# Two state-space layers, one core: second delta and second projection of the next scan moved beside the output pipeline, with DVE additions

## The chip, the cores and the metric

One core of one Trainium2 chip runs the whole batch of 8 images. The metric is the time of one execution on the device in microseconds (us), the median of several runs. The engines are PE (matrix products into PSUM, with PEld for its weight loads), DVE (vector), ACT (scalar functions and copies), POOL (GpSimd, elementwise here) and SP, which issues nearly all DMAs of this kernel. Every engine and SP work through their own queue in order.

## The reference

Two layers follow each other on x of shape (8, 64, 64, 96). Both normalise by groups, project to 2 x 192 channels, convolve 3x3 by channel, apply SiLU, scan the 4096 positions in four directions, normalise over channels, gate with SiLU(z), project back to 96 and add x. Layer 0's scan is the expensive one:

```
xs    = cross_scan(xc)                       # 4 directions: rows, columns, both reversed
x_dbl = einsum('bkdl,kcd->bkcl', xs, x_proj_w)   # 6 delta rows, 16 B rows, 16 C rows
delta = softplus(x_dbl[:, :, :6] projected to 192 channels + dt_projs_b)
dA    = exp(delta * A)                       # A: 192 channels x 16 states per direction
h     = dA * h + delta * B * u               # along 4096 positions
y     = sum over 16 states (h * C) + u * D
y     = layernorm(merge of the 4 directions); out = x + (y * silu(z)) @ out_proj_w.T
```

Layer 1 is the same in shape, with shared weights for the directions and a scan in closed form, of which only the first 160 positions of each direction contribute (a check at the end falls back to a general form).

## The kernel before

**Tiling.** Channels lie on partitions in two halves (h = 0, 1) of 96, positions in pieces of T = 1024. The scan of an image runs over 4 directions x 4 pieces = 16 *units*; a unit has 2 *jobs* (one per half), a job 3 groups of 32 channels, a group 4 *sets* of 128 partitions (32 channels x 4 states). That is 768 wide instructions `tensor_tensor_scan` on DVE per image, each 128x1024. For images 1 to 7 a short unit (24 short sets) follows that serves layer 1 of the image before.

**What a job needs.** `projection` (per unit) multiplies xc with the projection weights into 78 rows, `take` copies them out of PSUM, and a DMA stores them (x_dbl); `replicate` reads B and C rows back, each broadcast to 128 partitions (512 KB a transfer). `ready` (per job) makes delta as a softplus in two parts: `argument` (2 matmuls from the first 7 rows of x_dbl), `parts` (Relu and Abs), `exponential`, `rounded` and `rounding` (the rounding error of 1 + z, by two Identity passes), `logarithm`; then `total` adds the four terms z, dtu, ln and dt on PE as products with the unit matrix (4 per half tile, 8 per job), `delta` copies the sum back into `ln`, POOL's `product` makes delta x u, `store` writes both to DRAM, and `fetch` reads them back broadcast (dt_rep, dtu_rep). For units of the reversed directions `low_rows` reads the 7 rows back from DRAM instead of projecting again.

**Order inside the scan.** `scan_rows` writes the order by hand: step n issues one set's instructions for every engine, set n's scan on DVE, set n+1's decay on ACT, set n+5's fetch on SP, and so on, and then the stages of `plan[n]`. Steps -5 to -1 fill the pipe. Job m+2 and unit m/2+2 are prepared while job m runs, so two jobs and two units must be ready at the beginning: job 0 and unit 0 come from outside (`first_delta`), job 1 and unit 1 are made by `early_steps` in steps -5 to 1 of the scan itself.

**Order between scans.** `between(b, y)` runs `out_phase` on one or two streams of 8 chunks: the finish of layer 0 of image b and, from b = 1, the finish of layer 1 of image b-1, whose input y1 `short_sum` reads back from DRAM (8 loads), scales on ACT and patches on DVE. A chunk passes fixed lags: sum (0), mean on PE and `centre` on DVE (1), `square` (2), variance (3), gates and SiLU (7), `row` and `scale` (8), affine and product (9), output projection and `end` (10). After each step's stages come those of `plan[k]`, filled by `put(step, stage)`. Beside the chunks the plan holds: the four loads of the next image's xc, the first projection and first delta of the next scan (`first_delta`, steps 3 to 18), the statistics of x of image b+2 (`piece` loads and `chunk_stats`, then the three stages of a group norm at steps 10, 11, 14) and the group norm of layer 1 (18, 19, 20). Every fourth step also has `newton` on DVE and `roots` on ACT for the inverse deviation. PSUM tiles of `mean`, of `weights` and of all beside work share two banks. Image 0 has no pipeline before it: `begin` runs the same stages one after the other.

SP issues loads and stores of all these stages in one queue.

Of the kernel before, what the change touches and what calls it, by code (L numbers as in the profile page):

```python
# [10 lines left out]
ALU = mybir.AluOpType  # L11
# [36 lines left out]
def two_ss2d_layers(ctx: ExitStack, tc: tile.TileContext, t: dict, out: bass.AP):  # L48
# [352 lines left out]
    def scan_rows(xc, y, parts, plan, beside):  # L401

        with (
            tc.tile_pool(name="piece", bufs=1) as piece,
            tc.tile_pool(name="work", bufs=2) as work,
            tc.tile_pool(name="pslot", bufs=2, space=PSUM) as pslot,
            tc.tile_pool(name="pdrive", bufs=1, space=PSUM) as pdrive,
            tc.tile_pool(name="pacc", bufs=1, space=PSUM) as pacc,
            tc.tile_pool(name="pmisc", bufs=1, space=PSUM) as pmisc,
        ):
            units, jobs, sets, x_dbl = parts  # L420
            total = len(sets)
            plan = plan(pmisc)
            with tc.manual_schedule():
                low_rows(x_dbl, units[0], piece)
                state = None

                stages = ready(xc, x_dbl, jobs[1], piece, pmisc)
                stages += projection(xc, x_dbl, units[1], piece, pmisc)
                early_steps = (-5, -5, -5, -5, -4, -4, -4, -3, -3, -2, -2, -1, 0, 1)
                for step, (_, stage) in zip(early_steps + (-4, -3, -3, -2), stages):  # L430
                    plan.setdefault(step, []).append(stage)
                for n in range(-AHEAD, max(total + 4, max(plan, default=0) + 1)):
                    at = lambda i: sets[n + i] if 0 <= n + i < total else None
                    m, j = divmod(n + 1, PER)
                    if j == 0 and 0 <= m < len(jobs):

                        stages = []
                        if m + 2 < len(jobs):
                            prepare = short_ready if jobs[m + 2]["unit"]["short"] else ready
                            stages += prepare(xc, x_dbl, jobs[m + 2], piece, pmisc)  # L440
                        if m % NH == 1 and m // NH + 2 < len(units):
                            unit = units[m // NH + 2]
                            project = short_projection if unit["short"] else projection
                            stages += project(xc, x_dbl, unit, piece, pmisc)
                        for step, stage in stages:
                            plan.setdefault(n + step, []).append(stage)
                    fetch(at(AHEAD), work)
                    replicate(at(AHEAD_BC), x_dbl, work)
                    if at(0) and at(0)["unit"]["nth"] == 0 and at(0)["first"]:
                        state = piece.tile([P, D // GC * NS], F32, name="state0", bufs=2)  # L450
                    advance_set(at(0), state, work)
                    keep_state(at(-1))
                    fill(at(1), pslot)
                    if n % NS == NS - 2:
                        drive(at(2), pdrive)
                    release(at(-4), y, beside)
                    gate(at(1), work)
                    read_out(at(-1), work)
                    early(at(2), work)
                    collect(at(-3), xc, y, pacc)  # L460
                    for stage in plan.pop(n, []):
                        stage()
                assert not plan
# [26 lines left out]
    def low_rows(x_dbl, unit, piece):  # L490

        k, t0 = unit["k"], unit["t0"]
        unit["x_dbl"] = piece.tile([2 * ROWS, T], F32, name="x_dbl0")
        src = x_dbl[k % 2][k // 2 * ROWS :, t0 : t0 + T]
        nc.sync.dma_start(unit["x_dbl"][: R + 1, :], src[: R + 1, :])
# [36 lines left out]
            (4, lambda: take(1)),  # L532
        ]

    def ready(xc, x_dbl, job, piece, pmisc):

        unit, h = job["unit"], job["h"]
        k, t0, col = unit["k"], unit["t0"], unit["column"]
# [46 lines left out]
        def delta(s):  # L585
            nc.scalar.copy(job["ln"][:, halves[s]], job["ps"][:C, :])  # L586
            if s == SUB - 1:
                job["dt"] = job["ln"]

        def product():  # L590
            nc.gpsimd.tensor_tensor(  # L591
                like(job["dtu"], col),
                like(job["dt"], col),
                positions(xc[:, h, :], col, t0, T),
                ALU.mult,
            )

        def store():
            for c in ("dt", "dtu"):
                job[f"{c}_far"] = dram.tile([C, T], F32, name=f"{c}_far", bufs=3)  # L600
                nc.sync.dma_start(job[f"{c}_far"], job[c])

        return [
            (0, lambda: argument(0)),
            (1, lambda: parts(0)),
# [3 lines left out]
            (4, rounded),  # L609
            (5, rounding),  # L610
            (6, logarithm),
            (10, lambda: total(0)),
            (11, lambda: delta(0)),
            (11, lambda: total(1)),
            (12, lambda: delta(1)),
            (13, product),
            (15, store),
        ]
# [935 lines left out]
                chunk_stats(st, i, piece)  # L1554
        return group_norm(st, bank)

    def first_delta(b, xc, pool, pfirst):

        units, jobs, sets, x_dbl = parts = scan_parts(b)
        stages = projection(xc, x_dbl, units[0], pool, pfirst)  # L1560
        stages += ready(xc, x_dbl, jobs[0], pool, pfirst)
        return parts, [stage for _, stage in stages]

    def begin():

        with tc.tile_pool(name="pfirst", bufs=2, space=PSUM) as pfirst:
            bank = lambda name: pfirst.tile([P, MM], F32, tag="mm", name=name)
            xc = keep.tile([C, NH, L], F32, name="map")
            with tc.tile_pool(name="first", bufs=1) as pool:
                norm0[0] = conv_first(t["x"][0], xc, pool, bank)  # L1570
            with tc.tile_pool(name="before", bufs=1) as pool:
                parts, stages = first_delta(0, xc, pool, pfirst)
                for stage in stages:
                    stage()
            if NB > 1:
                norm0[1] = first_norm(1, bank)
        return xc, parts
# [11 lines left out]
    def short_sum(b, pool, put):  # L1589

        y1 = pool.tile([C, NH, L], F32, name="y1")
        ys = pool.tile([C, NH, HN], F32, name="ys")

        def load(h, i):
            at = slice(i * T, (i + 1) * T)
            nc.sync.dma_start(y1[:, h, at], xc1_far[b][:, h, at])

        def scale(h, i):
            at = slice(i * T, (i + 1) * T)
            nc.scalar.mul(y1[:, h, at], y1[:, h, at], w["dsum1"][:, h : h + 1])  # L1600

        def patch(h):
            for k, at, dst in segments(y1[:, h, :]):
                part = shaped(ys[:, h, k * HEAD + at.start : k * HEAD + at.stop], dst)
                nc.vector.tensor_tensor(dst, part, dst, ALU.add)

        put(0, nc.sync.dma_start, ys, ys_far[b])
        for h in range(NH):
            for i in range(NT):
                put(0, load, h, i)  # L1610
                put(4 + 2 * h + i // 2, scale, h, i)
            put(6 + h, patch, h)
        return y1

# [12 lines left out]
    def between(b, y):  # L1627
# [3 lines left out]
        with (  # L1631
# [11 lines left out]
            if b >= 1:  # L1643
                streams.append(second_of(b - 1, pool, put))
            for i in range(1, NT):
                put(7 + i, load, i)
            found = {}

            def beside(pmm):
                bank = lambda name: pmm.tile([P, MM], F32, tag="mm", name=name)  # L1650
                found["parts"], stages = first_delta(b + 1, xc, before, pmm)
                steps = (3, 4, 4, 5) + (5, 6, 6, 7, 10, 11, 11, 14, 15, 16, 16, 17, 17, 18)
                for step, stage in zip(steps, stages, strict=True):
                    put(step, stage)
                stages, found[1] = group_norm_stages(st, bank)
                for step, stage in zip((18, 19, 20), stages):
                    put(step, stage)
                if b + 2 < NB:
                    ahead = stats_tile()
                    pieces = []  # L1660

                    def piece(i):
                        pieces.append(before.tile([C, MM], F32, name="x_st", bufs=3))
                        nc.sync.dma_start(pieces[i], t["x"][b + 2][:, i * MM : (i + 1) * MM])

                    for i in range(L // MM):
                        put(i, piece, i)
                        put(i + 2, lambda i: chunk_stats(ahead, i, pieces[i]), i)
                    stages, found[0] = group_norm_stages(ahead, bank)
                    for step, stage in zip((10, 11, 14), stages):  # L1670
                        put(step, stage)
                return plan

# [163 lines left out]
```

## Time and profile before

| what | value | from |
|---|---|---|
| median of 3 runs | 12977.52 us (12971.58 to 12991.91) | times |
| the profiled execution | 13001.91 us, span of its instructions 13000.0 | times, page |
| busy, share of the span | DVE 87%, POOL 83%, ACT 75%, PE 75% | page, part 1 |
| granted TensorE clock, mean | 0.785 | table of cores |
| output pipelines behind images 0 to 7 | 82.8, 166.7, 164.2, 164.1, 163.6, 164.6, 145.4, 124.0 us | table by stage |
| one scan instruction 128x1024, one product set x B on DVE | 2.35 and 1.18 us | page, part 5 |

Busy time counts instructions at work; the mean over the span mixes the scans, where DVE and POOL are full, with the stretches between them. The times of the pipelines run from the first y_sum (line 1480) to the last result on DVE (line 1583 or 1531). The page's chain of waits holds only the very last pipeline and says nothing on the seven passages from image to image.

### The profile page before, as it was taken

The numbers are of one execution on the slowest core, as the hardware profiler recorded it, in microseconds if no ns is written. First come the engines' busy times: TensorE is split into PE (matmuls) and PEld (weight loads), VectorE is DVE, ScalarE is ACT, GpSimd is POOL, SyncE is SP. The second block draws the span as 40 slices with busy tenths as digits, with TensorE's granted clock in tenths as the row PEclk, the third lists the DMA queues.
The fourth block names the chain that finished last, engine by engine and source line by source line (L and its number), as shares of the span: only waits on it lengthen the run. The fifth ranks groups of instructions, "written<-read, shape, count | busy, mean of one in ns | idle before, by whom it ended". The sixth has DMA issues, their size and how long they took to land. (4 is left out here: it accounts for less than half of the span.)

```text
span 13000.0 us, 135568 instructions
## 1 busy us (share of the span) xinstructions
PE 9704.7 (75%) x44540; PEld 3050.4 (23%) x44540; DVE 11319.6 (87%) x7485; ACT 9795.9 (75%) x14884; POOL 10736.0 (83%) x4883
## 2 busy tenths in 40 slices
PE   6875688876888678876788867888588785886556
PEld 2221222222222222222222212222122221222112
DVE  6999799996999969999699996999869998799976
ACT  4788688776787768877688776887678886788864
POOL 4999798985999859898699976999769997799964
PEclk8887787877887778787788777888688886887766
DMA  3444444443444434444344434444344444344430
GB/s 98 159 159 153 131 161 155 158 148 100 161 157 158 145 107 162 151 159 140 119 161 158 157 123 124 161 158 157 119 125 161 157 162 129 132 160 156 155 96 25
DMA packets 654249, 1839.49 MB, mean 141 GB/s; under 512 B 174856, under 2 KB 178318, under 8 KB 653437
## 3 DMA queue, kind: packets, MB, share of 16 engines
q1 hardware_dynamic: 653533, 1830.73, 42.1%
q8 instruction: 353, 5.78, 0.2%
q14 instruction: 363, 2.97, 0.1%
HBM read 1524.94 MB, written 305.52 MB: 141 GB/s over the span
## 5 line engine op out<-in xcount | busy, mean ns | idle before, releaser
L842 POOL TENSOR_TENSOR out<-set,c_rep 128x1024 f32<-128x1024 f32 x3240 | 7471.5, 2326 | 941.2 <-PE acc L866 315.9
L825 DVE TENSOR_TENSOR_SCAN set<-decay,state,set 128x1024 f32<-128x1024 f32 x2304 | 5366.1, 2345 | 430.1 <-ACT decay L780 209.5
L780 ACT ACTIVATE decay<-dt_rep,w_a 128x1024 f32<-128x1024 f32 x3240 | 3553.1, 1097 | 559.5 <-DVE set L825 319.5
L814 DVE TENSOR_TENSOR set<-drive,b_rep 128x1024 f32<-128x1024 f32 x2430 | 2865.7, 1179 | 103.8 <-ACT drive L797 88.2
L866 PE MATMUL acc<-out,w_gather 128*32 128x256 f32 x25920 | 2398.8, 482 | 544.6 <-ACT y_short L886 393.5
L934 PE MATMUL ps_conv<-edged,taps 96*96 96x512 f32 (+1 forms) x4032 | 2461.4, 750 | 28.2 <-ACT z L558 26.0
L804 POOL TENSOR_TENSOR set<-dtu_rep,b_rep 128x1024 f32<-128x1024 f32 (+1 forms) x810 | 1898.5, 2344 | 56.0 <-DMA dt_far<-ln 29.8
L825 DVE TENSOR_TENSOR_SCAN set<-decay,set 128x1024 f32<-128x1024 f32 x768 | 1744.0, 2286 | 212.1 <-ACT decay L780 132.4
L857 PE MATMUL acc<-map,w_eye 96*32 96x256 f32 x4608 | 565.5, 572 | 1480.0 <-ACT map L897 1245.9
L897 ACT COPY map<-acc 32x256 f32<-32x256 f32 x3072 | 1471.0, 479 | 48.8 <-PE acc L866 8.6
L866 PEld LDWEIGHTS acc<-out,w_gather 128*32 128x32 f32 x25920 | 841.4, 132 | 2528.5 <-issue 1474.0
L591 POOL TENSOR_TENSOR dtu<-ln,map 96x1024 f32<-96x1024 f32 x256 | 670.5, 2619 | 481.4 <-ACT ln L586 303.1
L934 PEld LDWEIGHTS ps_conv<-edged,taps 96*96 96x96 f32 (+1 forms) x4032 | 722.4, 199 | 1362.7 <-issue 1209.0
L836 ACT COPY state<-set 128x1 f32<-128x1 f32 x2304 | 426.2, 185 | 753.9 <-DVE set L825 746.5
L577 PE MATMUL ps_sp<-z,w_eye 96*96 96x512 f32 x1024 | 700.5, 772 | 341.3 <-ACT ln L586 257.9
L797 ACT COPY drive<-dtu_rep 128x1024 f32<-128x1024 f32 (+1 forms) x810 | 797.0, 984 | 15.4 <-DVE set L814 10.9
L545 PE MATMUL ps_dt<-x_dbl,w_dtw 7*96 7x512 f32 x1024 | 590.3, 657 | 189.8 <-ACT z L558 157.3
L577 PE MATMUL ps_sp<-dtu,w_eye 96*96 96x512 f32 x1024 | 605.1, 676 | 0.7 <-ACT dtu L572 0.7
L577 PE MATMUL ps_sp<-ln,w_eye 96*96 96x512 f32 x1024 | 578.9, 650 | 0.0
L586 ACT COPY ln<-ps_sp 96x512 f32<-96x512 f32 x512 | 297.4, 581 | 347.8 <-PE ps_sp L577 340.7
L857 PEld LDWEIGHTS acc<-map,w_eye 96*32 96x32 f32 x4608 | 101.3, 121 | 1934.9 <-ACT map L897 1635.7
L577 PE MATMUL ps_sp<-dt,w_eye 96*96 96x512 f32 x1024 | 543.2, 613 | 0.0
(224 smaller groups left out, 9645.6 us busy)
## 6 DMA issues: line engine op xcount, KB each, us to landing
dt_rep<-dt_far SPq DMA_DIRECT2D x768, 512.0 KB, 4.0
dtu_rep<-dtu_far SPq DMA_DIRECT2D x768, 512.0 KB, 5.2
b_rep<-x_dblr SPq DMA_DIRECT2D x256, 512.0 KB, 7.7
c_rep<-x_dblr SPq DMA_DIRECT2D x256, 512.0 KB, 7.3
b_rep<-x_dblc SPq DMA_DIRECT2D x256, 512.0 KB, 8.0
c_rep<-x_dblc SPq DMA_DIRECT2D x256, 512.0 KB, 6.8
dt_far<-ln SPq DMA_DIRECT2D x256, 384.0 KB, 3.6
dtu_far<-dtu SPq DMA_DIRECT2D x256, 384.0 KB, 3.0
```

Of the source, the lines that this page charges most:

```text
L577: nc.tensor.matmul(job["ps"][:C, :], w["eye"], job[term][:, halves[s]], start=i == 0, stop=i == 3,)
L591: nc.gpsimd.tensor_tensor(like(job["dtu"], col), like(job["dt"], col), positions(xc[:, h, :], col, t0, T), ALU.mult,)
L780: nc.scalar.activation(s["decay"], s["group"]["dt"], AF.Exp, scale=rate)
L797: nc.scalar.copy(s["group"]["drive"], s["group"]["dtu"])
L804: nc.gpsimd.tensor_tensor(s["buf"], s["group"]["dtu"], b, ALU.mult)
L814: nc.vector.tensor_tensor(s["buf"], s["group"]["drive"], b, ALU.mult)
L825: nc.vector.tensor_tensor_scan(ordered(s["buf"], unit), ordered(s["decay"], unit), ordered(s["buf"], unit), 0.0 if unit["nth"] == 0 else s ...
L842: nc.gpsimd.tensor_tensor(s["out"], s["buf"], s["unit"]["c", s["i"]], ALU.mult)
L857: nc.tensor.matmul(acc, lhs[:, GC * g : GC * (g + 1)], positions(old[:, h, :], unit["column"], unit["t0"] + at, n), start=True, stop=False ...
L866: nc.tensor.matmul(acc, w["gather"], s["out"][:, at : at + n], start=s["i"] == 0 and unit["short"], stop=s["i"] == NS - 1, skip_group_chec ...
L897: nc.scalar.copy(yk, like(acc, unit["column"]))
L934: nc.tensor.matmul(job["ps"][:C, :], taps[l][:k, h, tap, :], edged[:k, tap // 3 : tap // 3 + rows, tap % 3 : tap % 3 + WW], start=tap == 0 ...
```

## The change

`first_delta` becomes `first_deltas`: beside the output pipeline it now makes the first projection, the first delta, the second delta and the second projection. In all deltas made there `ready(..., by_pe=False)` replaces the four stages `total(0)`, `delta(0)`, `total(1)`, `delta(1)` by one, `sums`, three additions on DVE. `scan_rows` loses `early_steps`; it reads the 7 rows of the second unit's x_dbl back from DRAM (`low_rows`, first stage of step -1). Later deltas inside the scan still go by PE. In the pipeline, the loads of `short_sum` move from step 0 to 1 and 2, its scalings to other steps, the loads of xc from 8, 9, 10 to 8, 10, 12, the pieces of x and their statistics six steps back, and their group norm to steps 16, 17, 18.

```diff
@@ scan_rows
-                low_rows(x_dbl, units[0], piece)
                 state = None
-
-                stages = ready(xc, x_dbl, jobs[1], piece, pmisc)
-                stages += projection(xc, x_dbl, units[1], piece, pmisc)
-                early_steps = (-5, -5, -5, -5, -4, -4, -4, -3, -3, -2, -2, -1, 0, 1)
-                for step, (_, stage) in zip(early_steps + (-4, -3, -3, -2), stages):
-                    plan.setdefault(step, []).append(stage)
+                plan.setdefault(-1, []).insert(0, lambda: low_rows(x_dbl, units[1], piece))
@@ ready
-    def ready(xc, x_dbl, job, piece, pmisc):
+    def ready(xc, x_dbl, job, piece, pmisc, by_pe=True):
...
+        def sums():
+            z, ln = job["z"], job["ln"]
+            nc.vector.tensor_tensor(z, z, job["dtu"], ALU.add)
+            nc.vector.tensor_tensor(ln, ln, z, ALU.add)
+            nc.vector.tensor_tensor(ln, ln, job["dt"], ALU.add)
+            job["dt"] = ln
...
-            (10, lambda: total(0)),
-            (11, lambda: delta(0)),
-            (11, lambda: total(1)),
-            (12, lambda: delta(1)),
+            *(in_pe if by_pe else [(10, sums)]),
@@ first_delta(s)
-        stages += ready(xc, x_dbl, jobs[0], pool, pfirst)
+        for job in jobs[:NH]:
+            stages += ready(xc, x_dbl, job, pool, bank, by_pe=False)
+        stages += projection(xc, x_dbl, units[1], pool, bank)
@@ short_sum
-        put(0, nc.sync.dma_start, ys, ys_far[b])
+        put(1, nc.sync.dma_start, ys, ys_far[b])
         for h in range(NH):
             for i in range(NT):
-                put(0, load, h, i)
-                put(4 + 2 * h + i // 2, scale, h, i)
+                put(1 + h, load, h, i)
+                put(5 + h + i // 3, scale, h, i)
             put(6 + h, patch, h)
@@ between
-                put(7 + i, load, i)
+                put(6 + 2 * i, load, i)
...
-                steps = (3, 4, 4, 5) + (5, 6, 6, 7, 10, 11, 11, 14, 15, 16, 16, 17, 17, 18)
+                steps = (2, 3, 3, 4) + (4, 5, 5, 6, 6, 7, 7, 10, 11, 12, 13)
+                steps += (12, 13, 13, 14, 14, 15, 15, 18, 19, 20, 21) + (14, 15, 15, 16)
...
-                        put(i, piece, i)
-                        put(i + 2, lambda i: chunk_stats(ahead, i, pieces[i]), i)
+                        put(i + 6, piece, i)
+                        put(i + 8, lambda i: chunk_stats(ahead, i, pieces[i]), i)
...
-                    for step, stage in zip((10, 11, 14), stages):
+                    for step, stage in zip((16, 17, 18), stages):
```

The second line of `steps` belongs to the second delta (11 stages from `argument(0)` at 12 to `store` at 21, with `sums` at 19) and to the second projection (14 to 16); in the first line `sums` of the first delta is at 11.

More of the change, by code (lines that the diff above doesn't have):

```diff
@@ L601, in store @@
                 nc.sync.dma_start(job[f"{c}_far"], job[c])
+        in_pe = [
+            (10, lambda: total(0)),
+            (11, lambda: delta(0)),
+            (11, lambda: total(1)),
+            (12, lambda: delta(1)),
+        ]
         return [
@@ L1555, in first_norm, with first_deltas @@
         return group_norm(st, bank)
-    def first_delta(b, xc, pool, pfirst):
+    def first_deltas(b, xc, pool, bank):
         units, jobs, sets, x_dbl = parts = scan_parts(b)
-        stages = projection(xc, x_dbl, units[0], pool, pfirst)
-        stages += ready(xc, x_dbl, jobs[0], pool, pfirst)
+        stages = projection(xc, x_dbl, units[0], pool, bank)
+        for job in jobs[:NH]:
+            stages += ready(xc, x_dbl, job, pool, bank, by_pe=False)
+        stages += projection(xc, x_dbl, units[1], pool, bank)
         return parts, [stage for _, stage in stages]
@@ L1571, in begin @@
             with tc.tile_pool(name="before", bufs=1) as pool:
-                parts, stages = first_delta(0, xc, pool, pfirst)
+                parts, stages = first_deltas(0, xc, pool, pfirst)
                 for stage in stages:
@@ L1650, in beside @@
                 bank = lambda name: pmm.tile([P, MM], F32, tag="mm", name=name)
-                found["parts"], stages = first_delta(b + 1, xc, before, pmm)
-                steps = (3, 4, 4, 5) + (5, 6, 6, 7, 10, 11, 11, 14, 15, 16, 16, 17, 17, 18)
+                found["parts"], stages = first_deltas(b + 1, xc, before, pmm)
+                steps = (2, 3, 3, 4) + (4, 5, 5, 6, 6, 7, 7, 10, 11, 12, 13)
+                steps += (12, 13, 13, 14, 14, 15, 15, 18, 19, 20, 21) + (14, 15, 15, 16)
                 for step, stage in zip(steps, stages, strict=True):
```

## The prediction

> **What bounds the kernel now.** I read the page first (DVE busy 87% of the span, POOL 83%, both full inside the scans; every fifth slice or so is thinner), then the scans' first and last lines in the timeline, then a table by stage of the stretches between scans. Between the last short set of one image and steady scanning of the next lie an output pipeline (some 164 us) and a start of the scan (some 32 us). The change works only there: seven passages, five of them (behind images 1 to 5) alike. Two rows of the table, first the pipeline behind image 2, then the same stretch behind image 6, which has no image b+2 whose statistics it takes; columns: stretch, length, busy us and count of PE, PEld, DVE, ACT, POOL, granted clock, DMA share, GB/s.
>
> ```profile
> 4608.10:4772.30 164.20, 139.46 (x268) 41.67 (x268) 75.68 (x110) 98.44 (x131) 82.60 (x52) 0.81 0.35 96
> 11011.00:11156.40 145.40, 135.17 (x264) 40.72 (x264) 69.95 (x91) 96.68 (x128) 81.97 (x52) 0.84 0.37 97
> ```
>
> PE is the fullest engine, and 18.8 us hang on the statistics. The timeline of DVE shows where most of it goes: the third `centre` stands behind `chunk_stats`, whose piece of x queues behind eight loads of y1 (3.1 MB).
>
> ```profile
> 4613.76 1.22 DVE L1493 TENSOR_TENSOR map<-map,ps_mean 96x1024 f32<-96x1024 f32 x1 [0.49 <-PE ps_mean L1416]
> 4629.47 0.69 DVE L151 BATCH_NORM_STATS2 bn_st<-x_st 96x6 f32<-96x512 f32 x1 [14.49 <-DMA x_st<-in_x]
> ```
>
> The start of the scan, DVE again: after the pipeline's last result it waits twice, for `drive` and for the first `decay`; only from the third scan (4804.56) on does it run without a gap.
>
> ```profile
> 4771.62 0.69 DVE L1531 TENSOR_TENSOR x_in<-ps_out,x_in 96x512 f32<-96x512 f32 x1 [2.11 <-PE ps_out L1449]
> 4787.17 1.22 DVE L814 TENSOR_TENSOR set<-drive,b_rep 128x1024 f32<-128x1024 f32 x1 [14.86 <-ACT drive L797]
> 4797.54 2.29 DVE L825 TENSOR_TENSOR_SCAN set<-decay,set 128x1024 f32<-128x1024 f32 x1 [9.15 <-ACT decay L780]
> 4804.56 4.47 DVE L825 TENSOR_TENSOR_SCAN set<-decay,set 128x1024 f32<-128x1024 f32 x2
> ```
>
> Both waits are ACT's, which serves the second delta (L557 to L586) and the second projection (L517) ahead of `decay`. Call the end of 4771.62 + 0.69 = 4772.3 "E": the third scan starts at E+32.3.
>
> **Part 1, the transfers.** Pieces of x go from step i to i+6, y1 loads from step 0 to steps 1 and 2. Nothing holds SP between, so the loads still start near 4613.7 and need their 11.3 us; but the first reader is now `scale` on ACT at step 5. Behind image 6, where no piece stands in the way, the same DMAs flow and the fourth `centre` starts 14.9 us after the first y_sum instead of 25.4: **-10.5 us** remain at every later step up to 8 (bounds -8 and -14.5, the idle itself).
>
> **Part 2, the statistics' chain** (L162 to L175) moves from steps 10, 11, 14 to 16, 17, 18. Now it costs the rest, 18.8 - 10.5 - 1.3 (grown by step 9, left as it is) = 7.0 us: PE stands still for DVE twice and then runs at half clock:
>
> ```profile
> 4690.43 0.30 PE L175 MATMUL ps_gv<-gdev,w_group 96*96 96x1 f32 x2 [2.22 <-DVE gdev L173]
> 4690.59 1.74 PE L1416 MATMUL ps_mean<-y_sum,w_avg 96*96 96x512 f32 x2
> ```
>
> The last figure is 1.08 at full clock. At 16 and 17 the two waits (1.8 and 2.2) stay, the clock's share may not: 4.0 for 7.0, **-3** (0 to -5).
>
> **Part 3, second delta and projection into the pipeline.** Moved per image: 2 `argument` and 4 projection matmuls, 4 half-tile Relu/Abs (0.58), Exp, Ln and two Identity (1.06 each), 2 `take` (0.68), POOL `product` (2.35), three stores (384, 384, 312 KB). Removed from the pipeline: 8 matmuls of the first delta's `total` and 2 copies; from the start of the scan 8 more and 2.
> PE: the two `total` blocks behind image 6 held the next `mean` back 3.4 us each, -6.8; added 2 x 1.06 (L545 at 4773.59) + 4 x 0.97 (L506 at 4792.41, full clock) = 6.0. But projection product(0) now stands on PE behind parts(1) at step 14, where ACT also has the roots and their tables (2 x 1.28), and product(1) behind Identity, Identity, take(0). I take 2.6 us of PE waiting (0 to 6): **+1.8** (-1 to +5). ACT's extra 6.8 us (4 x 0.58 + 4 x 1.06 + 2 x 0.68 - 2 x 0.58) sits in a stretch with 66 idle us; for Exp at step 6, in front of `parts` and PE's bank, **+1** (0 to 3). Stores: DMA share there is 0.35, nothing; without that cover 1.08 MB at 300 GB/s, 3.6.
>
> **Part 4, the sums on DVE.** Three additions of 96x1024 per delta. 1.22 us each by L1493, 3.66 per delta. But both operands are in SBUF, and the only such row in this pipeline is L1411, 0.69 us alone:
>
> ```profile
> L1411 DVE SCALAR_TENSOR_TENSOR r<-p,r x32: 691/1280/2819, 1497.7 to 12968.8; 128x512 f32<-128x512 f32 x32
> 4744.87 2.59 DVE L1411 SCALAR_TENSOR_TENSOR r<-p,r 128x512 f32<-128x512 f32 x1
> 4744.57 2.35 POOL L1489 TENSOR_TENSOR y<-y,sz 96x1024 f32<-96x1024 f32 x1 [4.38 <-ACT y L1464]
> ```
>
> DVE's instruction ends 0.55 us after POOL's: it waited POOL out. So an addition costs 1.22 to 1.22 + 2.35, three of them 3.66 to 10.7, both deltas 7.3 to 21.4. L1122, with two operands in SBUF while POOL stood still, took 0.814 for 640 elements, no wait at all. [...]
> What it costs the path: at step 11 `centre`, `scale` and the matmul of `weights` are behind it, and PE has some 3 us in hand: **+2** (0 to 5). At step 19 the variance of the second statistics stands behind it on DVE, and behind that ps_gv on PE, which already waits 1.56 there; behind PE the rest of the pipeline's tail. Sums 3.66 plus one POOL product would be 6.0; POOL has only one product per step there, so I take **+4.5** (2 to 10.7, PE at half clock after such a wait would be included). [...]
>
> **Part 5, the start of the scan.** What goes: Relu to `take` on ACT before `decay`, PE's half-clock totals. Then `decay` waits only for its transfer, as would set 0 at about E+12.5: a gain of 13. But x_dbl of the second unit now comes by DMA (low_rows, 28 KB), which SP issues at step -1 behind dt, dtu, edged, eight replicas and the next group's dt and dtu; argument of the third delta on PE, and on ACT its parts(0), which stand ahead of the decay of set 2, wait for it. Bytes: 4 x 0.52 + 0.22 + 8 x 0.52 = 6.5 MB. The sixth replica, 4.4 MB in, landed 9.0 us after 4781.06, at 4790.1; the other 2.1 MB at the 325 GB/s of 4780 to 4790 take 6.5: 4796.6. Then argument 2.0 (half clock), parts 1.17, state 0.19, decay 1.12: third scan at 4801.1 instead of 4804.6, with DMA's best slices 4800: **-4** (-2 to -13; if the replicas share the queues unevenly the small transfer can land early). What is late next is DVE itself: full from there.
>
> **The sum.** Behind images 1 to 5: -10.5 - 3 + 1.8 + 1 + 2 + 4.5 - 4 = -8.2, five times, -41. Behind image 6 parts 1 and 2 have nothing to give: +5.3. Behind image 0 (one stream, 82.8 us) the second delta ends after the pipeline: Ln with table 2.3, sums 3.7, product 2.35, store 3, some 6 later than today's store, on which `edged` (POOL waited 4.9 for it at L1011) and SP's queue depend; less part 5: +2 (-4 to 8). First image: both deltas run one after the other, one buffer each. Today the last store lands at 162.6. Then: second Identity 147.6, sums 151.3, product and store 156.7; second delta Relu/Abs and Exp with table by 155.9, Identities (they need the stored buffer) 158.8, Ln 161.1, two more additions, product, store 169; less part 5: +4 (0 to 8). Total **-30 us** on an execution of 13001.91 (span 13000.0 and 1.9 around it). The median of the runs is 12977.52, 24.4 below the profiled one; I subtract from the median: 12948.
>
> **Rivals.** (a) Slower: DVE's addition at step 19 (and 11) holds PE. The sum is -69 without it and 6 x S with S for both sums, 6.5 taken; S = 11.5 gives nothing, from 15.9 on it is slower by 0.2%. Bound 21.4 plus half clock; with S = 17.5 it is +36, 13014. For: L1411, ps_gv's present wait. Against: POOL is busy only half the time there. (b) No change: low_rows and the reordered loads give less; parts 1 and 5 at their poor ends (-8, -2) are +2.5 and +2 on five, +2 at three more starts: -1, 12976. For: both are bound by the same bytes as before. Against: nothing reads y1 before step 5. (c) More: set 2 doesn't wait for low_rows: 7 x -9, -93, 12885. For: ACT and PE are otherwise free there. Against: queues empty in order in the record (4.4 MB before the sixth replica landed).
>
> **From cases to numbers.** Forecast 0.46, (a) 0.27, (b) 0.17, (c) 0.10. The likeliest one's own range is 12910 to 12975; with (c) and most of (a) it is 12870 to 13025. The bound of 0.2% (26 us) is about what can be told from no change here. The forecast lies close to it: 0.37 of its 0.46 count as faster, 0.09 as same. With (a) 0.02, 0.01, 0.24, (b) 0.04, 0.10, 0.03 and (c) 0.10 faster: faster 0.53, same 0.20, slower 0.27.
>
> **What would show it.** Right: no idle before bn_stats at the pipeline's start; third scan at E+28; additions at steps 11 and 19 longer than 1.22 where POOL runs; ps_gv at step 19 waiting some 5 us. Wrong: y1's loads holding ACT at step 5; third scan at E+32; a pipeline longer than 164 us behind images 1 to 5; PE's clock at 0.5 in the tail.

## The result and the profile after

The changed kernel took 12965.11 us (median of 12 runs, 12936.07 to 13008.93), the kernel before 12968.16 us (12 runs on the same chip, 12936.60 to 12991.91). The ratio is 1.0001 with a 95% interval of 0.9987 to 1.0015: no difference that can be measured. The forecast of -30 us (0.9977) lies outside that interval, the forecast's range holds the time.

The profiled execution of the changed kernel had a span of 13004.9 us. The stages that the change touches can be read from it far more sharply than from the medians (us; before, then after, both from the profiled execution):

| stage | before | after |
|---|---|---|
| third scan of image 0, from the start | 205.0 | 210.6 |
| pipeline behind image 0 | 82.8 | 83.4 |
| pipelines behind images 1 to 5, mean | 164.6 | 166.6 |
| pipeline behind image 6 | 145.4 | 152.1 |
| E to the third scan, behind images 1 to 6, mean | 32.5 | 28.3 |
| these stages and the start behind image 0 (-0.3), all images added up | | -2.6 |
| the scans between these stages, image by image | | -10 to +27 |

A pipeline counts from the first y_sum on POOL to the last result on DVE (E). An image has 384 wide scan instructions (16 units of 2 jobs of 12 sets), not 768. The scans differ between these two executions by such amounts, with either sign; that is noise around the stages, whose cause was not pursued, and it goes with runs of one kernel that lie 24 to 85 us apart. The pipelines have a noise of their own: behind images 2 and 4 of this one execution they take 168.0 and 163.8 us, and the two are 3.4 us apart already at chunk 3, ahead of all that the additions delay. In the same 10 us of both (from 35.6 us after the first y_sum) the granted clock is 0.50 behind image 2 and 1.00 behind image 4. So the 2.0 us by which the mean of the pipelines has grown can't be told from none.

The table by stage for the changed kernel, behind images 2 and 6 (columns as before: stretch, length, busy us and count of PE, PEld, DVE, ACT, POOL, granted clock, DMA share, GB/s):

```profile
4594.90:4762.85 167.95, 136.90 (x264) 41.49 (x264) 89.77 (x116) 104.16 (x139) 85.41 (x53) 0.84 0.36 100
11008.70:11160.80 152.10, 129.33 (x260) 39.31 (x260) 81.96 (x97) 102.08 (x136) 85.13 (x53) 0.87 0.37 100
```

PE, still the fullest engine, has less to do than before (136.9 us for 139.5), DVE 14 us more (89.8 for 75.7), and yet the stretch behind image 2 is longer (168.0 for 164.2).

Line numbers of the pipeline are 7 higher than before. **The early stall is gone.** On DVE's timeline the third `centre` stands at 9.6 us after the first y_sum, with a short wait for PE only; 22.8 were the mean before. First the row of before (behind image 2, 22.0 us after its first y_sum), then that of the changed kernel:

```profile
4630.08 1.20 DVE L1493 TENSOR_TENSOR map<-map,ps_mean 96x1024 f32<-96x1024 f32 x1
...
4604.51 1.22 DVE L1500 TENSOR_TENSOR map<-map,ps_mean 96x1024 f32<-96x1024 f32 x1 [2.79 <-PE ps_mean L1423]
```

The `scale` of each chunk, as a mean over the five pipelines, shows what became of that lead (us from the first y_sum; number of the chunk):

| | 0 | 3 | 4 | 9 | 10 | 11 | 12 | 15 |
|---|---|---|---|---|---|---|---|---|
| before | 57.9 | 76.1 | 86.2 | 124.9 | 130.8 | 139.7 | 143.5 | 156.4 |
| after | 39.4 | 58.7 | 69.7 | 107.7 | 116.9 | 130.3 | 143.1 | 157.9 |
| ahead by | 18.5 | 17.4 | 16.5 | 17.2 | 13.9 | 9.4 | 0.4 | -1.5 |

Chunk 11 is scaled at step 19 and chunk 12 at step 20. The lead of 17 us lasts to step 17 and is lost between steps 18 and 20. The additions are only one part of what lies there; the statistics that were moved to steps 16 to 18 are another, and the kernel no_sums below tells them apart. The timeline of all engines behind image 2:

```profile
4728.23 1.21 DVE L589 TENSOR_TENSOR z<-z,dtu 96x1024 f32<-96x1024 f32 x1
...
4729.34 2.33 POOL L1496 TENSOR_TENSOR y<-y,sz 96x1024 f32<-96x1024 f32 x1 [3.31 <-ACT y L1471]
4729.48 3.28 DVE L590 TENSOR_TENSOR ln<-ln,z 96x1024 f32<-96x1024 f32 x1
4732.79 1.22 DVE L591 TENSOR_TENSOR ln<-ln,dt 96x1024 f32<-96x1024 f32 x1
...
4734.09 2.33 POOL L595 TENSOR_TENSOR dtu<-ln,map 96x1024 f32<-96x1024 f32 x1 [2.42 <-DVE gm L169]
4734.11 2.33 DVE L171 TENSOR_TENSOR gdev<-bn_mv,gm 96x1 f32<-96x1 f32 x1
...
4736.87 0.48 PE L175 MATMUL ps_gv<-gdev,w_group 96*96 96x1 f32 x2 [12.12 <-DVE gdev L173]
4737.21 2.00 PE L1428 MATMUL ps_r<-r,w_pick 128*96 128x512 f32 x2
```

The three additions take 5.71 us on DVE. The second stands still while POOL runs its product (3.28 for the 1.21 of the first; it ends 1.09 after POOL's L1496). Then the product of the second delta (L595) starts the moment its last addition is done, and now a 96x1 subtraction (L171) takes 2.33 us, to within 0.02 of the end of POOL's instruction; at 4710.79 the same line took 0.16. Behind it PE has waited 12.12 us for ps_gv (the same in all five pipelines), where it waited 1.56 before, and then runs at half clock: 2.00 for a pair of matmuls that takes 1.02 to 1.08 at full clock. The row of 4710.79, and the ps_gv of before behind image 2:

```profile
4710.79 0.16 DVE L171 TENSOR_TENSOR gdev<-bn_mv,gm 96x1 f32<-96x1 f32 x1
...
4749.89 0.33 PE L175 MATMUL ps_gv<-gdev,w_group 96*96 96x1 f32 x2 [1.56 <-DVE gdev L173]
```

At step 11, the first delta's sums in the same view:

```profile
4657.02 2.28 DVE L589 TENSOR_TENSOR z<-z,dtu 96x1024 f32<-96x1024 f32 x1
...
4659.33 3.25 DVE L590 TENSOR_TENSOR ln<-ln,z 96x1024 f32<-96x1024 f32 x1
...
4662.62 1.22 DVE L591 TENSOR_TENSOR ln<-ln,dt 96x1024 f32<-96x1024 f32 x1
...
4665.62 0.80 PE L1405 MATMUL ps_zb<-gn_shift,zw 96*96 96x1 f32 x4 [2.80 <-DVE y L1500]
...
4666.76 1.99 PE L1423 MATMUL ps_mean<-y_sum,w_avg 96*96 96x512 f32 x2 [0.34 <-ACT zb L1406]
```

6.75 us on DVE, and PE waits 2.80 us and comes back at half clock. The granted clock of this stretch and of the one behind ps_gv (columns as in the table by stage) says so:

```profile
4665.62:4670.25 4.63, 4.29 (x9) 1.96 (x10) 4.18 (x5) 2.87 (x5) 4.03 (x4) 0.50 0.38 96
4736.87:4742.40 5.53, 5.53 (x8) 2.13 (x9) 1.22 (x1) 0.68 (x1) 0.00 (x0) 0.50 0.00 1
```

**The start of the scan** went as worked out. E is 4762.85; SP issues the small load of x_dbl behind the replicas, PE's `argument` waits for it, ACT's `parts` stand ahead of the third `decay`, and the third scan starts 28.6 us after E:

```profile
4777.16 0.28 SPq L489 DMA_DIRECT2D x_dbl<-x_dblr  x1
...
4787.26 1.99 PE L542 MATMUL ps_dt<-x_dbl,w_dtw 7*96 7x512 f32 x2 [25.13 <-DMA x_dbl<-x_dblr]
...
4789.28 0.59 ACT L554 ACTIVATE dt<-ps_dt 96x512 f32<-96x512 f32 x1 [11.52 <-PE ps_dt L542]
...
4790.33 1.12 ACT L787 ACTIVATE decay<-dt_rep,w_a 128x1024 f32<-128x1024 f32 x1
...
4791.48 2.29 DVE L832 TENSOR_TENSOR_SCAN set<-decay,set 128x1024 f32<-128x1024 f32 x1 [7.81 <-ACT decay L787]
```

### The profile page after: what moved, and what is told of

It is laid out like the page before. It is cut to its first block, busy times and chain, and to the rows that moved or that the text cites. A ratio compares the mean times of both kernels' runs of the same rounds, so it can differ in the third digit from the quotient of the medians.

```text
span 13004.9 us, 135020 instructions
## 1 busy us (share of the span) xinstructions
PE 9539.5 (73%) x44284; PEld 3007.5 (23%) x44284; DVE 11419.5 (88%) x7533; ACT 9753.2 (75%) x14841; POOL 10737.4 (83%) x4883
## 5 line engine op out<-in xcount | busy, mean ns | idle before, releaser
L595 POOL TENSOR_TENSOR dtu<-ln,map 96x1024 f32<-96x1024 f32 x256 | 670.1, 2618 | 284.1 <-DVE ln L591 139.9
L574 PE MATMUL ps_sp<-z,w_eye 96*96 96x512 f32 x960 | 660.7, 777 | 311.7 <-ACT ln L583 256.5
L574 PE MATMUL ps_sp<-dtu,w_eye 96*96 96x512 f32 x960 | 564.2, 673 | 0.0
L574 PE MATMUL ps_sp<-ln,w_eye 96*96 96x512 f32 x960 | 546.4, 654 | 0.0
L574 PE MATMUL ps_sp<-dt,w_eye 96*96 96x512 f32 x960 | 514.7, 619 | 0.0
L554 ACT ACTIVATE dt<-ps_dt 96x512 f32<-96x512 f32 x512 | 303.0, 592 | 273.5 <-PE ps_dt L542 254.5
```

The costliest lines, as they stand in the source:

```text
L574: nc.tensor.matmul(job["ps"][:C, :], w["eye"], job[term][:, halves[s]], start=i == 0, stop=i == 3,)
L595: nc.gpsimd.tensor_tensor(like(job["dtu"], col), like(job["dt"], col), positions(xc[:, h, :], col, t0, T), ALU.mult,)
```

## The experiments

Theory A, from these rows: the transfers and the start gain what they should, and DVE's additions take it back. Theory B: the tail is held by the two statistics' chains anyway, and the lead would be lost without any addition. All kernels below ran with before on the same chip; the pipelines and starts are from their profiled executions.

| kernel | median us | before us | ratio (95%) | pipelines 1 to 5 | image 6 | E to third scan |
|---|---|---|---|---|---|---|
| changed kernel | 12965.11 | 12968.16 | 1.0001 (0.9987 to 1.0015) | 166.6 | 152.1 | 28.3 |
| transfers_only | 12925.41 | 12978.54 | 0.9956 (0.9939 to 0.9973) | 154.0 | 139.8 | 33.4 |
| no_sums | 12874.25 | 12978.54 | 0.9910 (0.9891 to 0.9930) | 151.6 | 142.2 | 28.8 |
| sums_late | 12968.65 | 12978.54 | 0.9985 (0.9972 to 0.9998) | 164.7 | 150.6 | 28.7 |
| rows_early | 12925.82 | 12978.54 | 0.9958 (0.9943 to 0.9972) | 164.7 | 151.6 | 20.6 |
| spread_end | 12967.01 | 12985.46 | 0.9985 (0.9974 to 0.9996) | 168.6 | 151.1 | 28.5 |
| spread_mid | 12928.65 | 12985.46 | 0.9945 (0.9925 to 0.9965) | 155.9 | 147.7 | 28.4 |
| spread_rows | 12867.25 | 12985.46 | 0.9910 (0.9895 to 0.9925) | 153.3 | 147.5 | 19.9 |

### transfers_only: parts 1 and 2 alone, on the kernel before

```diff
-        put(0, nc.sync.dma_start, ys, ys_far[b])
+        put(1, nc.sync.dma_start, ys, ys_far[b])
-                put(0, load, h, i)
-                put(4 + 2 * h + i // 2, scale, h, i)
+                put(1 + h, load, h, i)
+                put(5 + h + i // 3, scale, h, i)
-                put(7 + i, load, i)
+                put(6 + 2 * i, load, i)
-                        put(i, piece, i)
-                        put(i + 2, lambda i: chunk_stats(ahead, i, pieces[i]), i)
+                        put(i + 6, piece, i)
+                        put(i + 8, lambda i: chunk_stats(ahead, i, pieces[i]), i)
-                    for step, stage in zip((10, 11, 14), stages):
+                    for step, stage in zip((16, 17, 18), stages):
```

> The kernel before with parts 1 and 2 alone: the reordered transfers and the moved statistics, the first delta still summed by PE at its old steps, no second delta in the pipeline. Theory A (the early stall is gone for good, and in the changed kernel the DVE additions take it back later): pipelines behind images 1 to 5 go from a mean of 164.6 to about 150 us, nothing at image 6, so some -70 us in all, 0.9945 of before. Theory B (the pipeline's tail is held by the statistics' two chains, whatever comes before them): pipelines stay at 162 or more, ratio 0.999 or more. The start of the scan stays at E+32 under both.

Measured: 154.0 us, and 0.9956. The table by stage of this kernel, behind images 2 and 6:

```profile
4604.40:4764.10 159.70, 143.13 (x268) 42.83 (x268) 76.28 (x110) 98.01 (x131) 82.02 (x52) 0.80 0.38 98
10950.10:11089.90 139.80, 125.64 (x264) 38.92 (x264) 70.77 (x91) 96.39 (x128) 81.91 (x52) 0.90 0.39 101
```

The gain is kept to the end: -10.6 us in the mean, less than the -14.6 expected here. So theory B falls in its plain form. Three things were not expected. The start of the scan came at E+33.4 instead of E+32. Behind image 6, where no statistics are taken, the pipeline is 5.6 us shorter (139.8 for 145.4); behind image 0, with one stream, it is 7.9 us longer (90.7 for 82.8). That behind image 6 comes with a higher granted clock (0.90 for 0.84); what raised it was not pursued.

### no_sums: the changed kernel without its six additions

```diff
         def sums():
             z, ln = job["z"], job["ln"]
-            nc.vector.tensor_tensor(z, z, job["dtu"], ALU.add)
-            nc.vector.tensor_tensor(ln, ln, z, ALU.add)
-            nc.vector.tensor_tensor(ln, ln, job["dt"], ALU.add)
             job["dt"] = ln
```

> The changed kernel without the six DVE additions of the two deltas of the pipeline (delta stays the bare logarithm there: that part of the computation is left out). Theory A (the additions take the lead back): pipelines behind images 1 to 5 from a mean of 166.5 to about 147 us, 7 of it at steps 11 to 14 and 12 at steps 18 to 21, six pipelines, some -115 us, ratio 0.991 to before. Theory B (the tail is held by the statistics' chains anyway): pipelines at 160 or more, ratio 0.997 or more.

Measured: 151.6 us and 0.9910; theory A. That the total agrees to the digit is partly luck: the pipelines were expected at 147, and the start of the first image (202.9 us for 210.6) and the one behind image 0 (29.3 for 36.4) gave 14.8 us that were not expected.

The additions do not cost all of the 166.6 - 151.6 = 15.0 us. At chunk 3, scaled at step 11 ahead of the first addition, the changed kernel is already 2.6 us behind (58.7 against 56.1); no addition stands ahead of that point, and it is of the size of the noise of pipelines named above. From there to E it takes 107.8 us, and 95.5 without additions: **12.3 us in the mean of these five pipelines**, and 12.7 behind image 6 (95.2 against 82.5). In rows_early, a kernel below with the same pipelines, it is 107.7 or 107.8 again. Of the 12.3, 4.2 come from chunk 3 to chunk 9 (48.9 against 44.7), which is step 11's share, and 8.1 from chunk 9 to E (58.9 against 50.8). PE's timeline at step 19:

```profile
4695.16 0.33 PE L175 MATMUL ps_gv<-gdev,w_group 96*96 96x1 f32 x2 [4.25 <-DVE gdev L173]
```

The wait is 4.25 instead of 12.12 (in four of the five pipelines, 1.41 in the other). The difference, 7.87, is just the three additions (5.71) and what L171 lost to POOL's product behind them (2.33 - 0.15 = 2.18). But 4.25 is more than the 1.56 of before: the third stage of the other statistics, moved by part 2 to step 18, now stands right ahead on DVE and waits 2.23 us there for ACT, and `newton`'s third instruction (0.69 alone) takes 2.07.

How far each kernel is ahead of before at the `scale` of a chunk, in us:

| | 3 | 4 | 9 | 11 | 12 | 15 |
|---|---|---|---|---|---|---|
| transfers_only | 11.7 | 17.7 | 19.9 | 12.2 | 11.9 | 10.6 |
| no_sums | 19.9 | 25.9 | 24.1 | 15.2 | 14.4 | 13.5 |
| changed kernel | 17.4 | 16.5 | 17.2 | 9.4 | 0.4 | -1.5 |

So of the 18.7 us that the changed kernel loses behind chunk 9, no_sums loses 10.6 and transfers_only 9.3 without any addition. In before, PE's two waits for the statistics of x are over by chunk 4; in these kernels they stand at steps 16 and 17, right ahead of chunk 9 and behind it. That much of theory B holds; whether the moved statistics are all of that loss was not tested. The changed kernel's PE there:

```profile
4701.73 0.30 PE L164 MATMUL ps_gm<-bn_mv,w_group 96*96 96x1 f32 x2 [1.87 <-DVE bn_mv L162]
...
4711.47 0.30 PE L175 MATMUL ps_gv<-gdev,w_group 96*96 96x1 f32 x2 [2.22 <-DVE gdev L173]
```

### sums_late: the second delta's additions two steps later

```diff
-                steps += (12, 13, 13, 14, 14, 15, 15, 18, 19, 20, 21) + (14, 15, 15, 16)
+                steps += (12, 13, 13, 14, 14, 15, 15, 18, 21, 22, 23) + (14, 15, 15, 16)
```

> The changed kernel with the second delta's additions two steps later (21), its product and store at 22 and 23. Theory A (at step 19 they stand ahead of the variance of the statistics, for which PE waits): ps_gv at step 19 waits under 4 us instead of 12, pipelines behind images 1 to 6 some 10 us shorter, -60 us, ratio 0.9955 to before. Theory B (moved, they hold another wait of the same size, or the chains hold PE without them): pipelines within 3 us of the changed kernel's 166.5, ratio 0.998 or more.

Measured: ps_gv waits 4.25, as it should, and chunk 12 is scaled at 134.5 instead of 143.1, yet the pipelines end at 164.7. Theory A's place was right, its gain was not: the additions hold the next thing, as the rival says. On DVE, then PE:

```profile
4755.57 3.25 DVE L591 TENSOR_TENSOR ln<-ln,dt 96x1024 f32<-96x1024 f32 x1
```

```profile
4760.01 2.02 PE L1428 MATMUL ps_r<-r,w_pick 128*96 128x512 f32 x2 [3.32 <-DVE y L1504]
4761.82 3.62 PE L1456 MATMUL ps_out<-y,w_out 96*96 96x512 f32 x4
4766.31 3.70 PE L1456 MATMUL ps_out<-y,w_out 96*96 96x512 f32 x4 [0.87 <-DVE x_in L1538]
```

A `scale` behind the additions is late, PE waits 3.32 us, and from there to the end of this pipeline it runs at half clock (3.70 for four matmuls that took 1.88). Behind images 3 and 5 the same wait of 3.32 us stands there, but the clock is back for the last two groups of matmuls; these pipelines took 163.7 and 163.8 us, the other three 164.1, 167.9 and 164.0.

### rows_early: the small load ahead of the replicas

```diff
-                plan.setdefault(-1, []).insert(0, lambda: low_rows(x_dbl, units[1], piece))
+                low_rows(x_dbl, units[1], piece)
```

> The changed kernel with the small load of x_dbl issued ahead of the replicas instead of behind them. My theory of the start (parts(0) of the third delta on ACT waits for that load and holds the decay of set 2): the third scan at E+21 instead of E+28.5 behind every image, 7 x -7 = -50 us, ratio 0.996 to before; pipelines unchanged. Rival (the replicas themselves or drive and PE hold the third scan): E+27 or later, ratio 0.999 or more.

Measured: the third scan at E+20.6 in the mean, 0.9958, pipelines like the changed kernel's (164.7 for 166.6; one of the five takes about 168 us here, three in the changed kernel). The timeline of all engines, with E at 4744.6:

```profile
4743.95 0.27 SPq L489 DMA_DIRECT2D x_dbl<-x_dblr  x1
...
4745.92 1.06 PE L542 MATMUL ps_dt<-x_dbl,w_dtw 7*96 7x512 f32 x2 [2.05 <-DMA x_dbl<-x_dblr]
...
4764.50 2.29 DVE L832 TENSOR_TENSOR_SCAN set<-decay,set 128x1024 f32<-128x1024 f32 x1
```

`argument` now runs 1.3 us after E instead of 24.4, and the third scan no longer waits at all (7.81 before). The position of one load of 28 KB in SP's queue was worth 7.7 us per image.

### spread_end and spread_mid: one addition per step, in two positions

Both kernels put the three additions of a delta into three steps (the remainder is summed into dtu, so that the first of them need not wait for the logarithm). spread_end leaves each as the last work of its step:

```diff
+        def rest():
+            nc.vector.tensor_tensor(job["dtu"], job["z"], job["dtu"], ALU.add)
+        def with_rest():
+            nc.vector.tensor_tensor(job["ln"], job["ln"], job["dtu"], ALU.add)
+        def with_linear():
+            nc.vector.tensor_tensor(job["ln"], job["ln"], job["dt"], ALU.add)
+            job["dt"] = job["ln"]
...
-                steps = (2, 3, 3, 4) + (4, 5, 5, 6, 6, 7, 7, 10, 11, 12, 13)
-                steps += (12, 13, 13, 14, 14, 15, 15, 18, 19, 20, 21) + (14, 15, 15, 16)
+                steps = (2, 3, 3, 4) + (4, 5, 5, 6, 6, 7, 7, 10, 9, 11, 12, 12, 13)
+                steps += (12, 13, 13, 14, 14, 15, 15, 18, 16, 19, 20, 20, 21) + (14, 15, 15, 16)
```

spread_mid has the same steps, but issues the addition ahead of `end`:

```diff
                     for stage, lag in order:
+                        if stage is end:
+                            for extra in mids.pop(k, []):
+                                extra()
                         if 0 <= k - lag < n:
                             stage(k - lag)
```

> The changed kernel with the three additions of each delta in three different steps (9, 11, 12 and 16, 19, 20) instead of one, each still the last work of its step on DVE. The remainder z + dtu is kept in dtu, so that it need not wait for the logarithm. Theory A (an addition costs PE its time only where DVE has no idle stretch to take it; three in a row find none): shorter rows of waits, but each still ahead of the next step's centre or of the statistics, so pipelines behind images 1 to 5 at 158 to 162 us instead of 166.6. Rival C (only the sum of DVE's time counts, wherever it stands): 164 to 168.

> The same three steps, but each addition is put between scale and the last addition of the step (end), where DVE waits 3 to 5 us for ps_out from PE. Theory A: the additions are hidden there, pipelines behind images 1 to 5 at 152 to 156 us, close to the 151.6 without any additions; ps_gv at step 19 waits under 5 us; six pipelines by -12, some -70 us, ratio 0.9945 to before. Rival C: 164 or more, ratio 0.998 or more.

Measured: spread_end 168.6 us, no better than the changed kernel (a miss for theory A as I had put it); spread_mid 155.9 us and 0.9945. Work and steps are the same, so rival C, that DVE's time counts wherever it stands, falls too: what decides is where in the step the addition stands. DVE of spread_mid at step 16:

```profile
4707.73 1.21 DVE L1509 TENSOR_TENSOR y<-y,ps_r 96x1024 f32<-96x1024 f32 x1
4708.86 2.35 DVE L588 TENSOR_TENSOR dtu<-z,dtu 96x1024 f32<-96x1024 f32 x1
4712.03 0.69 DVE L1600 TENSOR_TENSOR x_in<-ps_out,x_in 96x512 f32<-96x512 f32 x1 [0.83 <-PE ps_out L1461]
```

Though it took 2.35 us, where L591 at 4743.43 took 1.21, the addition fits into the time that DVE would have waited for ps_out, and 0.83 is left. At the end of the step it stands instead ahead of the statistics and of the next `scale`. DVE of spread_end:

```profile
4719.34 2.11 DVE L171 TENSOR_TENSOR gdev<-bn_mv,gm 96x1 f32<-96x1 f32 x1
...
4732.11 1.87 DVE L187 TENSOR_TENSOR gn_p<-gn_r 96x1 f32<-96x1 f32 x1 [0.50 <-ACT gn_r L186]
4734.02 2.27 DVE L188 TENSOR_TENSOR gn_p<-gn_p,gv 96x1 f32<-96x1 f32 x1
```

Shifted behind the additions, even these small instructions take 1.87 to 2.27 us; at 4711.39 and 4711.58 L187 and L188 took 0.15 and 0.16. That they meet POOL's products here, as L171 does in the changed kernel, is an inference from their length. In spread_end ps_gv waited less than in the changed kernel, 4.50 or 7.38 us, but ps_gm at step 16 waited 4.71 instead of 1.87, behind the addition that now stands there. In spread_mid ps_gv still waited 7.38 us in three of the five pipelines and 1.75 in the two others, where under 5 was expected: where it waited longer, the mid position did not keep L171 from POOL's product of the chunk (2.15 us there).

### spread_rows: both causes removed

> spread_mid with the small load of x_dbl ahead of the replicas. If both causes are separate, their gains add: pipelines as in spread_mid, third scan at E+21, together some -125 us, ratio 0.9905 to before. If the earlier end of the pipeline only meets transfers that are not there yet, the third scan comes later than E+25 and the ratio stays above 0.993.

Measured: 12867.25 us, 0.9910; pipelines 153.3, third scan at E+19.9. The two gains add up (0.9945 x 0.9958 = 0.9903), and the kernel beats both the one before and the changed one.

## Why the prediction failed where it did

The predicted terms and what they measured, us per pipeline behind images 1 to 5 unless it says otherwise:

| step of the prediction | predicted | measured | from |
|---|---|---|---|
| parts 1 and 2, transfers and statistics | -13.5 | -10.6 | transfers_only against before |
| part 3, PE and ACT for the second delta | +2.8 | -2.4 | no_sums against transfers_only |
| **part 4, sums at step 11** | +2 | +4.2 | after against no_sums, chunk 3 to chunk 9 |
| **part 4, sums at step 19** | +4.5 | +8.1 | the same, chunk 9 to E |
| ahead of the first addition | 0 | +2.6 | the same, up to chunk 3; noise of pipelines |
| part 5, start of the scan | -4 | -4.0 | after against before |
| one such passage | -8.2 | -2.1 | -20.0 in starts, +9.6 in pipelines, over five |
| image 6 / image 0 / first image | +5.3 / +2 / +4 | +1.9 / +0.3 / +5.6 | stages |
| sum | -29.7 | -2.6 | stages |

**The step that failed is the price of part 4 on the path**: 6.5 us for both sums, 12.3 measured. Each share lies inside its own range (0 to 5, 2 to 10.7), but both in the upper half, and six passages pay them: 35 us more than forecast, and the whole forecast gain was 30. At step 11 the slack was about right ("some 3 us in hand": 6.75 us on DVE cost the path 4.2), but the additions were longer than +2 allows for, because POOL held two of the three (2.28 and 3.25 us for 1.22; they ended 1.09 and 1.08 after the instruction of POOL beside them). At step 19 the length was right (6.0 was worked out, 5.71 came), but 1.5 of it was to be hidden and nothing was, and L171 lost 2.18 us more. The diff and the rows of before could have told this: the product of the second delta is the next thing on POOL and meets the variance, whose instructions have two SBUF operands, as L1411 has (2.59 us in before with a product of POOL beside it, 0.69 alone). L1411, called the only such row of the pipeline, is not: L171 is another. "ps_gv at step 19 waiting some 5 us" became 12.12, of which 4.25 stand without additions too, because part 2 puts the third stage of the other statistics on DVE just ahead.

**Where the number was lucky.** The range holds 12965 us, but of the gain of 30 us only 3 came, less than the runs can tell from none, and the chances had put 0.53 on faster and 0.20 on no change. Part 3 came 5.2 us per pipeline better than forecast and so covers most of what part 4 cost in excess. And the median from which the forecast subtracts, 12977.52 of 3 runs, was 9 us above the 12968.16 of the 12 runs beside the result: from that one the same terms give about 12938, and the miss is 27 us instead of 17.

**Parts 1 and 2**: the stall went, and 10.6 of 13.5 us stayed. In transfers_only 11.7 us are there by chunk 3, about what part 1 was to give (10.5). Part 2 gave nothing that shows: at steps 16 and 17 the two waits are 1.87 and 2.22 us, 1.77 and 2.22 before, and the clock's share, which was to go, is there still (granted clock behind image 2 from 4702.20 to 4705.60 0.50, from 4712.50 to 4715.90 0.51). **Part 3** gave 2.4 us instead of costing 2.8: no_sums gains 8.2 us on transfers_only up to chunk 3 and loses 5.8 behind it. That the first comes from PE's `total` blocks that went away was not shown. The sum rests on two profiled executions, and single pipelines of one kernel differ by some 10 us, so its sign is not certain. **Part 5** was right in mechanism and size, and rows_early shows the mechanism by removing it.

**The rivals.** (a) named the right mechanism, and its price came out near the point where it put no gain: 12.3 us behind images 1 to 5 and 12.7 behind image 6, against 11.5. By (a)'s own sum that is -69 + 74 = +5 us, which the runs can't tell from no change. (b) has the right outcome and the wrong reason: transfers and start did not come at their poor ends. (c) is out: set 2 does wait for the load.

## What to carry to other kernels

Where two engines hand work to each other in every step, an addition on one of them is not priced by its duration but by its position: it is nearly free in front of an instruction that waits for the other engine anyway (4.3 us per pipeline for the six additions of spread_mid, 155.9 against 151.6), and costs its full length or more in front of the instruction for which the other one waits (8.1 us for 5.71 at step 19). Before a work item goes to "an engine with time left", list what stands behind it in that engine's order, who waits for that, and what its completion starts elsewhere. When a gain does not show in the total, compare the same point of the pipeline step by step. The step at which a lead vanishes tells where to look and not yet why: some half of what was lost here behind step 17 (9.3 and 10.6 of 18.7 us) was also lost in the kernels without the additions, and only those kernels could show it.

## What the runs showed of the hardware that was not expected

POOL's instruction holds up even DVE's smallest ones: L171, 96x1 with two SBUF operands, took 2.33 us in the changed kernel (4734.11, POOL's L595 from 4734.09) and 2.15 in spread_mid (4745.34, POOL's L1501 from 4745.14), instead of 0.15 or 0.16, and ended within 0.02 us of POOL's instruction both times. The `centre` at 4664.36, with one operand in PSUM, took 1.20 while POOL's L595 (4663.92, 2.35) was running, so it was not held.

In the clock records of the kernel before and of the changed kernel PE's granted clock was only ever 0.50 or 1.00, and every stretch at one of them (but for the last, cut off by the end) is a whole multiple of 3.41 us long. After the 2.80 us wait at step 11, shorter than any such stretch, it was 0.50. In sums_late behind image 2 it stayed there for the last 15.3 us, though PE was busy for 12.83 of them, with gaps of 0.87 us; behind image 3 of the same run it was back at 1.00 among the same groups with the same gaps (in the rows with a colon, granted clock in the last column but two):

```profile
4760.00:4775.30 15.30, 12.83 (x14) 3.45 (x14) 3.83 (x5) 3.02 (x4) 7.38 (x6) 0.50 0.30 90
...
6361.55 2.95 PE L1456 MATMUL ps_out<-y,w_out 96*96 96x512 f32 x4
6365.37 1.93 PE L1456 MATMUL ps_out<-y,w_out 96*96 96x512 f32 x4 [0.87 <-DVE x_in L1538]
6368.17 1.93 PE L1456 MATMUL ps_out<-y,w_out 96*96 96x512 f32 x4 [0.87 <-DVE x_in L1538]
...
6365.40:6370.80 5.40, 3.83 (x8) 1.08 (x8) 1.35 (x2) 0.00 (x0) 1.96 (x2) 1.00 0.71 219
```

What brings the full clock back these rows do not show: with gaps of 0.87 us it stayed away in one tail and came back in the other, and what decides between them was not pursued.
